# Turned features interleaved element by element, and one layer-0 vector held in a PSUM bank, in a four-layer graph-attention kernel

## The chip, the cores and the metric

The kernel runs on one core of a Trainium2 chip, in one launch. A core has five engines with instruction queues of their own: TensorE (PE: matrix products, results in PSUM), VectorE (DVE), ScalarE (ACT), GpSimd (POOL) and SyncE (SP), which here issues DMAs; 16 DMA engines move the data. SBUF is the working memory of 128 partitions, PSUM the small memory of 8 banks that TensorE writes. The metric is the device time of one execution in microseconds (us); lower is better.

## The reference

The input is 128 graphs of 128 nodes with 512 features each (`x`, float32) and a 0/1 adjacency matrix each (`adj`). Four layers follow, each `x = layernorm(x + attention(x, adj))`:

```
layer 0: scores = leaky(x.w_src + (x.w_dst)^T + b), softmax over neighbours, times x     (1 head, no projection)
layer 1: a two-stage attention: x @ W1 (512 x 1024, 4 heads of 256), elu, then @ W2 (1024 x 512, 1 head)
layer 2: 8 heads: x @ W (512 x 8*64), scores from a1 and a2, softmax, times the projection
layer 3: scores from x @ W_fc^T and W_attn, softmax, times x, elu                        (1 head)
```

All arithmetic is in float32.

## The kernel before

The kernel treats the graphs in pairs: 64 pairs, and `pair(n)` writes down the operations of one of them. `first` is layer 0, `second` and `third` are the two stages of layer 1, `fourth` is layers 2 and 3. Between them stand the projections with the weights `w1s`, `w2s` and `w3s`, which stay in SBUF.

Nothing is issued as it is written down. Each operation is a record with an engine, an estimated cost, the buffers that it reads and writes, and a due time. `plan` gives due times within a pair, spaced by `STRETCH`, and the pairs follow each other by `PACE`; `lay_out` then plays all engines forward in time by the estimated costs and writes out one fixed order for each engine's queue. It lets an operation run ahead of the oldest one not yet issued by at most `AHEAD`, gives out at most `BANKS` PSUM banks, counts a DMA by its cost and number of descriptors, and keeps DVE operations marked `port` from lying beside POOL's. Operations of several pairs are thus interleaved on each engine, and on the chip each engine works through its own fixed order, waiting on semaphores. `lay_out` also places the buffers in one SBUF `arena`.

A projection (`strassen`) multiplies the rows of two graphs by weights in seven block products instead of eight. Its left blocks, `left[g][a]`, are halves (a = 0 or 1) of the features of graph g, and four more are sums and differences of them that POOL makes (`sums`, line 853: eight of 128 x 256 in a pair for w1 and w3, four of 128 x 512 for w2). Three products use left blocks directly, four use the sums. Each block product is a chain of matmuls (line 829); each float32 matmul shows in the trace as two loads of weights (LDWEIGHTS, here the left block) and two MATMULs. A pair has 56, 56 and 28 such records for w1, w2 and w3. The other matmuls are L900 (attention times features, 12 records), L995 (32), L1057 (32) and L951 (2). The results leave PSUM by a copy (L837 on ACT, or L838 on DVE) or by an addition on DVE (L876).

TensorE needs the left operand with features on the partitions, so the features have to be turned. `turned` does it in three steps: DVE transposes blocks of 32 x 32 (line 726), one DMA writes them to DRAM (`scr`, line 730), and another reads them back with the blocks rearranged (line 734 or 739):

```python
op("SP", 0.7, lambda: nc.sync.dma_start(
    out=o.ap.rearrange("p h (q c) -> p h q c", q=4),
    in_=scr.ap.rearrange("p f -> (p f)").rearrange("(q p h c) -> p h q c", q=4, p=P, h=n),
), [scr], [o], dma=0.415 * n, desc=4 * P * n)
```

Each piece of this read is 32 float32, 128 bytes. The form with `ordered=True` turns the features of two graphs (8 tiles of 128 x 128, four for each graph) ahead of w1 and of w3: two calls in a pair. The first two pairs in layer 0, and the last one to three pairs in their later stages, are `quick`: they turn on TensorE (line 712) with a copy out of PSUM (line 720).

Layer 0's scores are four DVE instructions in a pair (line 940), two with `w0d` and two with `w0s`: each multiplies 128 x 512 features by a vector that is spread over all partitions, and sums. Both vectors are loaded into SBUF at the start by a DMA that repeats the row for every partition. Line 1023 adds `shift2` to two columns of scores, on DVE, before the scores of layer 1's second stage (line 753 on ACT, 766 on DVE).

Of the kernel before, what the change touches and what calls it, by code (L numbers as in the profile page):

```python
# [17 lines left out]
P = 128  # L18
# [7 lines left out]

STRETCH, PACE, AHEAD = 1.26, 44.3, 58.4
HOP = {"PE": 0.0, "DVE": 0.0, "ACT": 0.45, "POOL": 1.06, "SP": 2.0}
SEED, SPREAD = 1, 0.0
SETUP = (-36.3, -10.6, -19.3)  # L30
QUICK = (2, 0, 1, 2, 3)
FIRST, LAST = (-64.8, -62.4, -117.1, -110.8, -116.1), ()
BANKS, PRODUCTS = 8, 2
SEES = {"PE": 0.06, "DVE": 0.06, "ACT": 0.06, "POOL": 0.06, "SP": 0.0}
# [3 lines left out]
SLACK = 2.0  # L38
EXTRA = 0.2
FLEX = ("copy",)  # L40
REACH = 0.0
LOADS = (46.3, 7.8)

# [246 lines left out]
def tile_gat_stack(  # L290
# [65 lines left out]
    def lasting(shape, name):  # L356
        b = Buf("const", shape)
        b.ap = const.tile(shape, F32, name=name)
        return b
# [51 lines left out]

    begin[0] = SETUP[0]
    w0b = [lasting([P, F], n) for n in ("w0d", "w0s")]
    w0d, w0s = (b.ap for b in w0b)
    for b, w in zip(w0b, (w0_dst, w0_src)):
        load(-22, "ACT", lambda b=b: b.ap, w.partition_broadcast(P), b, 256)
    b0b = lasting([P, 1], "b0t")
# [218 lines left out]
    def part(b, *index):  # L636

        return b, lambda: b.ap[(slice(None), *index)]
# [3 lines left out]
    def spread(cols, split=1):  # L642
# [23 lines left out]
        for (b, col), k in cols:  # L666
            def turn(col=col, a=a, k=k):
                c, o = col(), sT.ap[:, a : a + k, :]
                if len(c.shape) > 2:
                    o = o.rearrange("p (a b) c -> p a b c", a=c.shape[1])  # L670
                nc.vector.transpose(o, c.unsqueeze(len(c.shape)).to_broadcast([*c.shape, 32]))

            op("DVE", 0.06 + 0.04 * k, turn, [b], joins=[sT])
            a += k
# [13 lines left out]
    def turned(srcs, n, moving=False, ordered=False):  # L688
# [3 lines left out]
        o = Buf(f"pt{n}", [P, 4, n, 32] if moving else [P, n, P])  # L692
        m = n // len(srcs)
        if quick[0]:
            for a, (b, src) in enumerate(srcs):
                if ordered:
                    own = Buf("own", [P, m, P])

                    def order(own=own, src=src, copy=(nc.vector.tensor_copy, nc.scalar.copy)[a % 2]):
                        copy(  # L700
                            own.ap.rearrange("p k (r b) -> p k r b", b=4),
                            src().rearrange("p k (b r) -> p k r b", b=4),
                        )

                    op(("DVE", "ACT")[a % 2], 0.06 + 0.137 * m, order, [b], [own])
                    b, src = own, lambda own=own: own.ap
                for lo in range(0, m, 4):
                    px, w = bank(), min(4, m - lo)

                    def flip(src=src, lo=lo, w=w, px=px):  # L710
                        for u in range(w):
                            nc.tensor.transpose(px.ap[:, u * P : (u + 1) * P], src()[:, lo + u, :], ident)  # L712

                    def taken(lo=a * m + lo, w=w, px=px, moving=moving, e=(lo // 4 + a) % 2):
                        if moving:
                            to = o.ap[:, :, lo : lo + w, :].rearrange("p q h c -> p h q c")
                            got = px.ap[:, : w * P].rearrange("p (h q c) -> p h q c", h=w, q=4)
                        else:
                            to, got = o.ap[:, lo : lo + w, :], px.ap[:, : w * P].rearrange("p (h i) -> p h i", h=w)
                        (nc.vector.tensor_copy, nc.scalar.copy)[e](to, got)  # L720

                    op("PE", 0.12 * w, flip, [b], [px])
                    op(("DVE", "ACT")[(lo // 4 + a) % 2], 0.06 + 0.137 * w, taken, [px], joins=[o])
            return o
        for a, (b, src) in enumerate(srcs):
# [19 lines left out]
    def attend(rows, src, mask, scaled=False):  # L745
# [33 lines left out]

        op("ACT", [0.4] * nh, prelu, [*dict.fromkeys(r[0] for r in rows), src[0]], [z])  # L780
        op("DVE", [0.24] * nh, masked, [z, mask[0]], [zz, nm])
        op("ACT", [0.387] * nh, exp, [zz, nm], [zz, rs])
# [10 lines left out]
    def norm(ys, plus=0.0):  # L793
# [8 lines left out]

        op("DVE", 0.15, both, [st], [mv])

# [31 lines left out]
    def copied(px, w, to, joins=(), outs=()):  # L836
        op("ACT", 0.04 + w / 1200, lambda: nc.scalar.copy(to(), px.ap[:, :w]), [px], outs, joins)  # L837
        either("copy", "DVE", 0.05 + w / 960, lambda: nc.vector.tensor_copy(to(), px.ap[:, :w]))  # L838

# [23 lines left out]
    def strassen(left, s, w, nk, wide, cols, to, out, ready):  # L863
# [11 lines left out]
        def added(px, u, g, h):  # L875
            op("DVE", 0.05 + wide / 960, lambda: nc.vector.tensor_add(to(g, h), px.ap[:, :wide], u.ap[:, :wide]), [px, u], joins=[out[g]])  # L876

# [27 lines left out]
    def resid(o, pa, ri, g, r):  # L905
        op("DVE", 0.645, lambda: nc.vector.scalar_tensor_tensor(
            out=o.ap, in0=pa.ap, scalar=ri.ap[:, g : g + 1], in1=r[1](), op0=ALU.mult, op1=ALU.add
        ), [pa, ri, r[0]], [o])
# [16 lines left out]
    def first(n):  # L925
# [11 lines left out]
        for s, wv, init in ((1, w0d, 0.0), (0, w0s, b0t)):  # L937
            for g in G:
                jk = Buf("junk", [P, F])
                op("DVE", 0.63, lambda g=g, s=s, wv=wv, init=init, jk=jk: nc.vector.tensor_tensor_reduce(  # L940
                    out=jk.ap, in0=x0.ap[:, g, :], in1=wv, scale=1.0, scalar=init, op0=ALU.mult, op1=ALU.add,
                    accum_out=sc0.ap[:, s, g : g + 1],
                ), [x0], [jk], joins=[sc0], uses=[*w0b, b0b], port=True)
            if s:
                rows = spread([(part(sc0, 1), 2)])
# [72 lines left out]
    def third(st, xl2):  # L1018
# [3 lines left out]
        rows = spread([(part(xl2, every, 0, F // 2), 2)])  # L1022
        op("DVE", 0.07, lambda: nc.vector.tensor_add(
            sc2.ap, xl2.ap[:, :, 1, F // 2], shift2.ap
        ), [xl2], [sc2], uses=[shift2], port=True)
        zz, ri = attend(rows, part(sc2), (m1, lambda h: m1.ap[:, h, :]))
# [8 lines left out]
    def fourth(n, st, xl3):  # L1035
# [10 lines left out]
        for g in G:  # L1046
# [4 lines left out]
            for q in range(2):  # L1051
# [21 lines left out]
            ), True)  # L1073
            op("DVE", 0.14, lambda g=g: nc.vector.tensor_reduce(
                out=sz.ap[:, g, :], in_=z3[g].ap[:, :, FO:].rearrange("p h s -> p s h"), op=ALU.add, axis=AX.X
# [29 lines left out]
        ), [y], [], dma=1.58, desc=2 * P)  # L1105

    quick = [False]

    def pair(n):
# [6 lines left out]
        xl = [Buf("xl1", [P, 2, N1]) for _ in G]  # L1116
        left = [[part(xT, slice(4 * g + 2 * a, 4 * g + 2 * a + 2)) for a in range(2)] for g in G]
        s = sums(left, [P, 2, P])
# [11 lines left out]
        xl3 = [Buf("xl3", [P, 2, C3]) for _ in G]  # L1130
        left = [[part(xT2, slice(4 * g + 2 * a, 4 * g + 2 * a + 2)) for a in range(2)] for g in G]
        strassen(left, sums(left, [P, 2, P]), w3s, 2, C3, slice(0, C3), lambda g, h: xl3[g].ap[:, h, :], xl3, wh_ready)
# [67 lines left out]
```

## Time and profile before

| | us |
|---|---|
| median of 3 runs | 2966.2 (2963.7 to 2967.05) |
| the profiled execution | 2964.05 |
| its span, first to last instruction | 2962.3 |
| PE busy | 2892.2 |
| PE loading weights (beside matmuls) | 2360.1 |
| DVE busy | 2762.8 |
| ACT busy | 2326.7 |
| POOL busy | 2213.1 |

The granted TensorE clock was 0.991 over the span. The DMA engines moved 588.18 MB in 1448819 packets, 1236740 of them under 512 bytes. A group row of the profile gives line, engine, operation, tiles and shapes, count, busy time, mean duration in nanoseconds of one instruction, and idle time before it with what ended it. Mean durations overlap where an engine pipelines, so they can be longer than the spacing of the instructions. A row of the chain of waits or of the timeline gives start, length, engine, line and how many instructions are merged in it.

### The profile page before, as it was taken

How to read it: one execution, taken by the hardware profiler on the slowest of the kernel's cores; microseconds unless marked ns; L12 is line 12 of the kernel's file. 1: busy time of each engine (PE TensorE's matmuls, PEld its weight loads, DVE VectorE, ACT ScalarE, POOL GpSimd, SP SyncE). 2: the span in 40 equal slices, each digit the busy share in tenths (PEclk: the TensorE clock that was granted, in tenths of full speed). 3: DMA queues.
4: the chain of work that ended last, by engine and by line, in shares of the span. 5: the costliest groups of instructions: out<-in, count | busy, mean ns of one | idle time of the engine just before them, and what ended most of it. 6: DMA issues, size and time to landing. Idle time of an engine off the chain costs nothing. (4 is left out here: it accounts for less than half of the span.)

```text
span 2962.3 us, 56920 instructions
## 1 busy us (share of the span) xinstructions
PE 2892.2 (98%) x14292; PEld 2360.1 (80%) x14292; DVE 2762.8 (93%) x9694; ACT 2326.7 (79%) x7795; POOL 2213.1 (75%) x2855
## 2 busy tenths in 40 slices
PE   7999999999999999999999999999999999999997
PEld 4878788888888888888888888888888888888885
DVE  7789899999999999999999999999999999999976
ACT  3467788788788788788788788788778778778778
POOL 3877777777777877877877877877877877777854
PEclk9999999999999999999999999999999999999998
DMA  4369899999999999999999999999999999999851
GB/s 136 85 165 208 194 220 216 209 218 214 213 212 212 211 212 212 212 209 213 215 208 212 214 207 215 214 208 217 211 204 219 213 204 219 212 204 217 195 118 43
DMA packets 1448819, 588.18 MB, mean 199 GB/s; under 512 B 1236740, under 2 KB 1351172, under 8 KB 1448492
## 3 DMA queue, kind: packets, MB, share of 16 engines
q1 hardware_dynamic: 1447416, 582.97, 86.4%
q8 instruction: 116, 1.90, 0.3%
q14 instruction: 211, 1.73, 0.2%
q10 hardware_dynamic: 1076, 1.58, 0.2%
HBM read 363.68 MB, written 220.75 MB: 197 GB/s over the span
## 5 line engine op out<-in xcount | busy, mean ns | idle before, releaser
L829 PE MATMUL ps<-w2s,arena 128*128 128x257 f32 x3584 | 834.5, 384 | 3.6 <-DVE arena L1003 2.1
L829 PE MATMUL ps<-w1s,arena 128*128 128x258 f32 x3584 | 807.4, 383 | 6.5 <-DVE arena L876 3.2
L829 PEld LDWEIGHTS ps<-w1s,arena 128*128 128x128 f32 x3584 | 680.6, 190 | 162.1 <-issue 43.0
L775 ACT ACTIVATE arena<-arena,nm 128x128 f32<-128x128 f32 x1920 | 741.3, 389 | 62.2 <-DVE nm L766 58.5
L853 POOL TENSOR_TENSOR arena<-arena 128x256 f32<-128x256 f32 (+1 forms) x768 | 694.4, 922 | 114.2 <-DVE arena L1003 49.9
L829 PEld LDWEIGHTS ps<-w2s,arena 128*128 128x128 f32 x3584 | 667.8, 190 | 119.1 <-POOL arena L853 18.2
L753 ACT ACTIVATE ps<-arena 128x128 f32<-128x128 f32 x1480 | 538.7, 370 | 53.9 <-DMA arena<-row 15.0
L726 DVE STREAM_TRANSPOSE arena<-arena 128x512 f32<-128x512 f32 (+1 forms) x803 | 497.3, 630 | 24.8 <-ACT arena L775 4.6
L766 DVE CUSTOM_DVE_ANT_0 arena<-ps,arena 128x128 f32<-128x128 f32 x1850 | 501.8, 379 | 13.9 <-ACT ps L753 10.2
L829 PE MATMUL ps<-w3s,arena 128*128 128x273 f32 x1792 | 471.7, 398 | 20.7 <-DVE arena L876 16.5
L817 ACT ACTIVATE arena<-arena,mr,rd 128x512 f32<-128x512 f32 x512 | 393.7, 809 | 50.5 <-POOL mr L813 50.5
L829 PEld LDWEIGHTS ps<-w3s,arena 128*128 128x128 f32 x1792 | 322.2, 190 | 98.7 <-DVE arena L876 36.8
L837 ACT COPY arena<-ps 128x257 f32<-128x257 f32 (+2 forms) x577 | 205.4, 375 | 245.4 <-PE ps L829 245.1
L900 PE MATMUL ps<-arena 128*128 128x512 f32 x768 | 376.7, 602 | 3.2 <-DVE arena L720 2.9
L775 ACT ACTIVATION_READ_ACCUMULATOR arena<-arena,nm 128x1 f32 x1920 | 361.8, 188 | 0.0
L984 POOL TENSOR_TENSOR arena<-arena,b1t 128x512 f32<-128x512 f32 x256 | 349.8, 1371 | 10.8 <-DVE b1t L500 3.3
L797 DVE BATCH_NORM_STATS2 st<-arena 128x6 f32<-128x512 f32 x512 | 336.2, 678 | 9.3 <-POOL arena L1068 4.6
L876 DVE TENSOR_TENSOR arena<-ps,arena 128x258 f32<-128x258 f32 (+2 forms) x768 | 306.0, 412 | 35.3 <-PE ps L829 18.4
L812 POOL TENSOR_TENSOR md<-mv,rd 128x2 f32<-128x2 f32 x256 | 54.0, 211 | 374.3 <-ACT rd L807 357.3
L911 POOL TENSOR_SCALAR arena<-arena 128x256 f32<-128x256 int32 x256 | 292.2, 1141 | 54.8 <-DMA arena<-in_adj_dram 14.9
L766 DVE DVE_READ_ACCUMULATOR2_ANT nm<- 128x1 f32 x1850 | 278.5, 151 | 0.0
L1057 PEld LDWEIGHTS ps<-arena 128*128 128x128 f32 x2048 | 249.8, 194 | 33.9 <-issue 27.7
(97 smaller groups left out, 3952.8 us busy)
## 6 DMA issues: line engine op xcount, KB each, us to landing
scr<-arena SPq DMA_DIRECT2D x309, 512.0 KB
arena<-scr SPq DMA_DIRECT2D x309, 512.0 KB
arena<-row SPq DMA_DIRECT2D x185, 512.0 KB
arena<-in_x_dram SPq DMA_DIRECT2D x64, 512.0 KB
out_dram<-arena SPq DMA_DIRECT2D x64, 512.0 KB
arena<-row SPq DMA_DIRECT2D x185, 128.0 KB
scr<-arena SPq DMA_DIRECT2D x185, 128.0 KB
arena<-scr SPq DMA_DIRECT2D x185, 128.0 KB
```

Of the source, the lines that this page charges most:

```text
L726: op("DVE", 0.075 + 0.134 * m, lambda a=a, src=src: nc.vector.transpose(zb.ap[:, :, a * m : (a + 1) * m, :].rearrange("p b h c -> p h b c" ...
L753: nc.scalar.activation(z.ap[:, h * P : (h + 1) * P], rows[h][1](), AF.Prelu, bias=src[1]()[:, h : h + 1], alpha=SLOPE)
L766: nc.vector.tensor_tensor_reduce(out=zz.ap[:, h, :].rearrange("p (b a) -> p a b", b=4), in0=z.ap[:, h * P : (h + 1) * P].rearrange("p (a b ...
L775: nc.scalar.activation(zz.ap[:, h, :], zz.ap[:, h, :], AF.Exp, bias=nm.ap[:, h : h + 1], scale=-1.0, accum_out=rs.ap[:, h : h + 1],)
L797: op("DVE", 0.585, lambda g=g, y=y: nc.vector.bn_stats(st.ap[:, g, :], y()), [b], joins=[st])
L817: op("ACT", 0.715, lambda g=g, y=y: nc.scalar.activation(y(), y(), AF.Identity, bias=mr.ap[:, g : g + 1], scale=rd.ap[:, g : g + 1]), [b, ...
L829: nc.tensor.matmul(px.ap[:, :w], lhsT=lhs(k), rhs=rhs(k), start=(fresh and k == 0), stop=(k == nk - 1), skip_group_check=True,)
L853: op("POOL", cost, lambda: nc.gpsimd.tensor_tensor(out=own[o][1](), in0=a[1](), in1=b[1](), op=what), [a[0], b[0]], [s[o]])
L876: op("DVE", 0.05 + wide / 960, lambda: nc.vector.tensor_add(to(g, h), px.ap[:, :wide], u.ap[:, :wide]), [px, u], joins=[out[g]])
L900: op("PE", 0.885, lambda: nc.tensor.matmul(pa.ap.rearrange("p (s c) -> p s c", s=2) if paired else pa.ap, lhsT=pt.ap[:, h, :], rhs=xv[1]() ...
L911: op("POOL", 1.25, lambda: nc.gpsimd.tensor_scalar(out=m.ap, in0=a.ap, scalar1=0.0, scalar2=-BIG, op0=what, op1=ALU.mult), [a], [m])
L984: op("POOL", 1.255, lambda g=g, c=c: nc.gpsimd.tensor_add(xl[g].ap[:, c, : 2 * FH], xl[g].ap[:, c, : 2 * FH], b1t[:, c * 2 * FH : (c + 1) ...
```

## The change

- The turned features of one graph's `ordered` tiles are interleaved: instead of four tiles of 128 x 128 one after the other, the buffer is `[P, graph, node, k]` with the tile number k innermost. DVE's transpose writes that order (a step of four elements, 16 bytes, within a row), and the read from DRAM moves pieces of 128 elements, 512 bytes.
- The left blocks become views of this buffer (`halves`): both TensorE's loads of weights and POOL's sums read it at a step of 16 bytes. The quick form writes its copies at that step.
- `w0d` is no longer spread over SBUF by a DMA: its row is loaded, TensorE spreads it with a matmul against ones into a PSUM bank, and it stays there. `BANKS` falls from 8 to 7. The two line-940 instructions that use it are no longer marked `port`.
- Line 1023's addition becomes an ACT instruction.
- The planner's constants change: `PACE`, `AHEAD`, `EXTRA` and a number of estimated costs, so the order of all queues is made anew.

```diff
-STRETCH, PACE, AHEAD = 1.26, 44.3, 58.4
+STRETCH, PACE, AHEAD = 1.26, 44.0, 70.0
-BANKS, PRODUCTS = 8, 2
+BANKS, PRODUCTS = 7, 2
-EXTRA = 0.2
+EXTRA = 0.5
...
-    w0b = [lasting([P, F], n) for n in ("w0d", "w0s")]
-    w0d, w0s = (b.ap for b in w0b)
-    for b, w in zip(w0b, (w0_dst, w0_src)):
-        load(-22, "ACT", lambda b=b: b.ap, w.partition_broadcast(P), b, 256)
+    w0b = [Buf("const", [P, F]), lasting([P, F], "w0s")]
+    w0d = w0b[0].ap = psum.tile([P, F], F32, name="w0d")
+    w0s = w0b[1].ap
+    r0 = row(-22, "ACT", one_row(w0_dst), F)
+    load(-22, "ACT", lambda: w0s, w0_src.partition_broadcast(P), w0b[1], 256)
+    at(-20, "PE", 0.9, lambda: nc.tensor.matmul(w0d, lhsT=ones[0:1, :], rhs=r0.ap[0:1, :], start=True, stop=True), [r0], [w0b[0]])
...
+        if ordered:
+
+            zb, o = Buf(f"zb{n}", [P, 4, len(srcs), 32 * m]), Buf(f"pt{n}", [P, len(srcs), P, m])
...
+                        elif ordered:
+                            to, got = o.ap[:, lo // m].rearrange("p i k -> p k i"), px.ap[:, : w * P].rearrange("p (h i) -> p h i", h=w)
...
+        if ordered:
+            for a, (b, src) in enumerate(srcs):
+                op("DVE", 0.075 + 0.134 * m, lambda a=a, src=src: nc.vector.transpose(
+                    zb.ap[:, :, a, :].rearrange("p b (c k) -> p k b c", k=m),
+                    src().rearrange("p h (b c) -> p h b c", c=32),
+                ), [b], joins=[zb])
+            op("SP", 0.5, lambda: nc.sync.dma_start(
+                out=scr.ap, in_=zb.ap.rearrange("p b a e -> p (b a e)")
+            ), [zb], [scr], dma=0.05 + 0.19 * n, desc=P)
+            op("SP", 0.6, lambda: nc.sync.dma_start(
+                out=o.ap.rearrange("p a (q c) k -> p a q (c k)", q=4),
+                in_=scr.ap.rearrange("p f -> (p f)").rearrange("(q p a e) -> p a q e", q=4, p=P, a=len(srcs)),
+            ), [scr], [o], dma=0.22 * n, desc=4 * P * len(srcs))
+            return o
...
-        op("ACT", [0.4] * nh, prelu, [*dict.fromkeys(r[0] for r in rows), src[0]], [z])
-        op("DVE", [0.24] * nh, masked, [z, mask[0]], [zz, nm])
+        op("ACT", [0.345 if nh < 4 else 0.378] * nh, prelu, [*dict.fromkeys(r[0] for r in rows), src[0]], [z])
+        op("DVE", [0.234] * nh, masked, [z, mask[0]], [zz, nm])
...
-                ), [x0], [jk], joins=[sc0], uses=[*w0b, b0b], port=True)
+                ), [x0], [jk], joins=[sc0], uses=[w0b[1 - s], b0b], port=not s)
...
-        op("DVE", 0.07, lambda: nc.vector.tensor_add(
-            sc2.ap, xl2.ap[:, :, 1, F // 2], shift2.ap
-        ), [xl2], [sc2], uses=[shift2], port=True)
+        op("ACT", 0.2, lambda: nc.scalar.activation(
+            sc2.ap, xl2.ap[:, :, 1, F // 2], AF.Identity, bias=shift2.ap[:, 0:1]
+        ), [xl2], [sc2], uses=[shift2])
...
+    def halves(t):
+
+        return [[(t, lambda g=g, a=a: t.ap[:, g, :, 2 * a : 2 * a + 2].rearrange("p i k -> p k i")) for a in range(2)] for g in G]
...
-        left = [[part(xT, slice(4 * g + 2 * a, 4 * g + 2 * a + 2)) for a in range(2)] for g in G]
+        left = halves(xT)
...
-        left = [[part(xT2, slice(4 * g + 2 * a, 4 * g + 2 * a + 2)) for a in range(2)] for g in G]
+        left = halves(xT2)
```

Six further estimated costs of DVE and ACT operations change by up to 0.055 us.

More of the change, by code (lines that the diff above doesn't have):

```diff
@@ L23 @@
 FMAX = 3.0e38
-STRETCH, PACE, AHEAD = 1.26, 44.3, 58.4
-HOP = {"PE": 0.0, "DVE": 0.0, "ACT": 0.45, "POOL": 1.06, "SP": 2.0}
+STRETCH, PACE, AHEAD = 1.26, 44.0, 70.0
+HOP = {"PE":0.0,"DVE":0.0,"ACT":0.45,"POOL":1.06,"SP":2.0}
 SEED, SPREAD = 1, 0.0
-SETUP = (-36.3, -10.6, -19.3)
-QUICK = (2, 0, 1, 2, 3)
-FIRST, LAST = (-64.8, -62.4, -117.1, -110.8, -116.1), ()
-BANKS, PRODUCTS = 8, 2
+SETUP = (-36.3,-10.6,-19.3)
+QUICK = (2,0,1,2,3)
+FIRST, LAST = (-64.8,-62.4,-117.1,-110.8,-116.1), ()
+BANKS, PRODUCTS = 7, 2
 SEES = {"PE": 0.06, "DVE": 0.06, "ACT": 0.06, "POOL": 0.06, "SP": 0.0}
@@ L38 @@
 SLACK = 2.0
-EXTRA = 0.2
+EXTRA = 0.5
 FLEX = ("copy",)
 REACH = 0.0
-LOADS = (46.3, 7.8)
+LOADS = (46.3,7.8)
 class Buf:
@@ L671, in turn @@
                 nc.vector.transpose(o, c.unsqueeze(len(c.shape)).to_broadcast([*c.shape, 32]))
-            op("DVE", 0.06 + 0.04 * k, turn, [b], joins=[sT])
+            op("DVE", 0.08 + 0.04 * k, turn, [b], joins=[sT])
             a += k
@@ L801, in both @@
                 nc.vector.bn_aggr(mv.ap[:, g, :], st.ap[:, g, :])
-        op("DVE", 0.15, both, [st], [mv])
+        op("DVE", 0.18, both, [st], [mv])
         def root():
@@ L836, in copied @@
     def copied(px, w, to, joins=(), outs=()):
-        op("ACT", 0.04 + w / 1200, lambda: nc.scalar.copy(to(), px.ap[:, :w]), [px], outs, joins)
-        either("copy", "DVE", 0.05 + w / 960, lambda: nc.vector.tensor_copy(to(), px.ap[:, :w]))
+        op("ACT", 0.05 + w / 1200, lambda: nc.scalar.copy(to(), px.ap[:, :w]), [px], outs, joins)
+        either("copy", "DVE", 0.065 + w / 960, lambda: nc.vector.tensor_copy(to(), px.ap[:, :w]))
     def project(lhs, wa, nk, w, n, to, t, ready):
@@ L875, in added @@
         def added(px, u, g, h):
-            op("DVE", 0.05 + wide / 960, lambda: nc.vector.tensor_add(to(g, h), px.ap[:, :wide], u.ap[:, :wide]), [px, u], joins=[out[g]])
+            op("DVE", 0.075 + wide / 960, lambda: nc.vector.tensor_add(to(g, h), px.ap[:, :wide], u.ap[:, :wide]), [px, u], joins=[out[g]])
         first = len(ops)
@@ L905, in resid @@
     def resid(o, pa, ri, g, r):
-        op("DVE", 0.645, lambda: nc.vector.scalar_tensor_tensor(
+        op("DVE", 0.7, lambda: nc.vector.scalar_tensor_tensor(
             out=o.ap, in0=pa.ap, scalar=ri.ap[:, g : g + 1], in1=r[1](), op0=ALU.mult, op1=ALU.add
@@ L1073, in fourth @@
             ), True)
-            op("DVE", 0.14, lambda g=g: nc.vector.tensor_reduce(
+            op("DVE", 0.09, lambda g=g: nc.vector.tensor_reduce(
                 out=sz.ap[:, g, :], in_=z3[g].ap[:, :, FO:].rearrange("p h s -> p s h"), op=ALU.add, axis=AX.X
```

## Prediction

> **What bounds the kernel now.** I read the page's busy rows first, for the engine with least room, then a table by windows for the steady middle.
>
> ```profile
> PE 2892.2 (98%) x14292; PEld 2360.1 (80%) x14292; DVE 2762.8 (93%) x9694; ACT 2326.7 (79%) x7795; POOL 2213.1 (75%) x2855
> q1 hardware_dynamic: 1447416, 582.97, 86.4%
> ```
> ```profile
> core 0: us, PE busy (x) PEld busy (x) DVE busy (x) ACT busy (x) POOL busy (x), PEclk, DMA share, GB/s
> 1044.00:1488.00 444.00, 439.86 (x2185) 360.56 (x2184) 429.77 (x1504) 360.87 (x1217) 341.64 (x441) 1.00 0.93 212
> ```
> Three resources are nearly full in the middle: PE 99%, DVE 97%, the DMA engines 93%; ACT (81%) and POOL (77%) have room. A busy PE row is modelled, so I take PE's true beat from the chain of waits, whose end is nearly all PE:
>
> ```profile
> 2699.74 2.11 PE ps L829 x8
> 2704.48 1.72 PE ps L900 x4
> 2706.20 2.62 PE ps L1057 x24
> 2715.82 8.70 PE ps L829 x40
> 2729.71 2.68 PE ps L995 x24
> 2732.39 1.85 PE ps L829 x8
> 2743.99 2.11 PE ps L829 x8
> ```
> The first and last lines are the same place one pair of graphs later: 44.25 us per pair. The beats: w1 products (x40) 217.5 ns, w3 (x8 at 2732) 231, L900 430 ns, L995 112 ns, L1057 109 ns; the w2 products, not shown, do 24 in 5.27 us, 220 ns. Per pair 56 x 0.2175 + 56 x 0.220 + 28 x 0.231 + 12 x 0.430 + 32 x 0.112 + 32 x 0.109 + 0.2 (L951) = 43.4 us. So PE has 0.85 us of idle in 44.25, and no change that leaves the matmuls alone can win more than 0.85 x 64 = 54 us in the steady part.
>
> Where the idle lies, the timeline shows at one of some 35 like places (the waits of the steady middle put 12.8 us in 35 times to this pair of lines):
>
> ```profile
> 1546.99 1.72 POOL L984 TENSOR_TENSOR arena<-arena,b1t 128x512 f32<-128x512 f32 x1
> 1547.51 0.43 DVE L876 TENSOR_TENSOR arena<-ps,arena 128x273 f32<-128x273 f32 x1
> 1547.87 1.40 DVE L940 CUSTOM_DVE_ANT_0 arena<-arena,w0s,b0t 128x512 f32<-128x512 f32 x1
> 1547.99 1.45 PEld L829 LDWEIGHTS ps<-w3s,arena 128*128 128x128 f32 x7 [0.79 <-DVE arena L876]
> 1547.99 1.65 PE L829 MATMUL ps<-w3s,arena 128*128 128x273 f32 x6 [0.39 <-DVE arena L876]
> ```
> Another L940, from 1545.91, had run 1.67 us beside POOL; L876 was queued behind it on DVE, and PE waited for L876. By groups:
>
> ```profile
> L940 DVE CUSTOM_DVE_ANT_0 arena<-arena,w0s,b0t 128x512 f32<-128x512 f32 x128 | 178.8, 1401 | 1.8 <-PE ps L375 1.8
> L940 DVE CUSTOM_DVE_ANT_0 arena<-arena,w0d 128x512 f32<-128x512 f32 x128 | 142.3, 1147 | 5.5 <-DMA arena<-in_x_dram 5.5
> L1023 DVE TENSOR_TENSOR sc<-arena,shift 128x2 f32<-128x2 f32 x64 | 26.2, 410 | 0.1
> L1003 DVE SCALAR_TENSOR_TENSOR arena<-arena,ps 128x512 f32<-128x512 f32 x256 | 167.4, 674 | 8.1 <-ACT arena L1002 8.1
> L853 POOL TENSOR_TENSOR arena<-arena 128x256 f32<-128x256 f32 x512 | 357.7, 715 | 50.1 <-DMA arena<-scr 15.5 <-ACT arena L775 12.1 <-DVE arena L876 5.1
> L1057 PEld LDWEIGHTS ps<-arena 128*128 128x128 f32 x2048 | 249.8, 194 | 33.9 <-issue 27.7 <-DVE arena L720 0.7 <-DVE ri L783 0.5
> ```
> L940, both inputs in SBUF, costs 1147 and 1401 ns, against 674 for L1003, as wide, with one input in PSUM. The extra is waiting for POOL: the w0d form's median is 692, so half its instances don't meet POOL at all.
>
> **The change part by part**, per pair unless said.
>
> DVE loses lock waits. With w0d in PSUM its two L940 have one SBUF input: 2 x (1147 - 690) = 0.91 us gone. L1023 leaves DVE: 0.41, of which about 0.26 was waiting (a tiny DVE instruction, L783, takes 150). ACT gets it at about 0.2 (L807: 203 ns); behind it on ACT stand only that layer's L753, which needed it anyway, and ACT idles 8 us a pair. The w0s pair stays: 2 x (1401 - 692) = 1.42 us of waits. So 1.17 of 2.59 us of waits go, 45%, and DVE falls by 1.3 us from 42.8 (429.77 of 444, times 44.25).
>
> Layout on DVE. The two ordered transposes (L726, 692 ns) now write at a 16-byte step. The nearest row is L766, which writes at a 128-byte step: the trace has it at 233 ns from start to start, and its unit-step twin L761 at 211. 22 ns per 128 elements is 88 per transpose, 0.18 a pair at most; at least 0, as nothing else in it changes. I take 0.1.
>
> DMA. The two reads back move 2048 pieces of 512 B instead of 8192 of 128 B. In the trace's packet records a 128 B packet takes 16.5 ns and one of 512 B 31.9: 8192 x 16.5 / 16 = 8.4 us against 4.1. The DMA share falls from 93% to about 84%. Of itself that is worth 0: in the middle PE waits for no DMA. SP's issues stay as many (about 0.6 us each), and fewer descriptors can only release SP earlier.
>
> TensorE's weights. Three of seven Strassen products (both left blocks and the last) load straight from the turned tile: 24 of w1's 56 loads and 12 of w3's 28 now step by 16 bytes. No load of before steps so. What a load costs today: L1057 moves 66 columns and L995 128, yet both beat at 109 to 112 ns, so there the load sets the beat and takes about 109; the 190 in the rows is latency. In the products it hides under 217.5 and 231. The Trainium skill, "SBUF — State Buffer", Specifications, speaks against the change: a 16-byte line needs two hits for full bandwidth, and here each element is alone on its line. At half rate a load takes about 2 x 107 + 2 = 216 ns: still under 217.5, so by this rule too the sum is 0, except where a strided load follows a short matmul (+0.1 each, up to 0.3 a pair). By the contiguous row it is 0. Below nothing it cannot be. If the cover goes, at three times, 24 x 110 + 12 x 96 = 3.8 us a pair. I take 0.05.
>
> POOL's sums (L853, eight of 256) now read both or one input at that step. The rows have only 715 ns contiguous; L1068, reading 64 of every 66, is no slower than its like. The skill's "GPSIMD Engine Reference", Performance pitfalls, gives about 50% more per element for steps over 8 bytes. By the row nothing; by the rule 0.36 each, 2.9 us of POOL (34.0 to 36.9 of 44), and the fourth sum 1.4 later. What hides it: near 1032 us the w1 products start at 1032.25, the one that uses the last sum comes 16 matmuls on, at 1035.73, and that sum is done by 1034.1: 1.6 us of room. Near 1004 and 1050 us the w3 sums have over 3. I take the rule, and it fits: 0 on the path. At double time (+2.8 us) PE would wait about 1.2 a pair.
>
> One PSUM bank goes for good: 7 are left for 3-bank products, two at a time, plus scores. The trace doesn't show a wait for a bank by name. From below 0; from above one more stall a pair like the 0.46 above. I take 0.05.
>
> The order. New costs, PACE, AHEAD and EXTRA let all queues be ordered anew, SP's and POOL's too; no row prices that. It can give back or take some tenths of a us a pair; I take 0 and keep it in the range.
>
> At the start w0d's broadcast becomes a 2 KB row, a matmul (L375, 0.8 us) and PE at a queue that already waits to 7.1 us: within 1 us either way. In the first two and last pairs the ordered copies (L720, 580 to 690 ns) write at the new step: under 1 us together.
>
> The sum. I read PE's idle as DVE's lateness, so that it shrinks as DVE's lost time does. DVE is freed of 1.17 us of waits and 0.15 of L1023's own work and given 0.1 for the transposes: 1.22 of 2.59, 47%. 0.47 x 0.85 = 0.40 us; less 0.05 for the loads and 0.05 for the bank, 0.30; over 64 pairs 19 us. The profiled execution was 2964.05 (span 2962.3, 1.75 around it), 2.15 under the median of the runs shown; so 2945 on its scale and 2947 on the median's.
>
> **Rivals.**
> (1) The loads bind: slower. Place: the 36 strided loads; it decides from 217 ns a load, twice today's, on. At three times +3.8 us a pair: about 3190; at 235 ns 24 x 17 + 12 x 4 = 0.46 a pair, +29 against the gain: about 2976. For: a step that leaves one element per line, and a margin of 1.5 ns at half rate. Against: [...]L766's writes show one line per element costing DVE almost nothing. 10% for a large loss, 8% for a small one.
> (2) Banks, or sums later than their room: PE waits 0.5 to 1.2 us a pair, less the gain: 2979 to 3024. For: PE's order is fixed, and one late operand stalls it. Against: ACT's and DVE's drains follow PE within a microsecond. 17%.
> (3) Nothing: the remaining stall is behind a w0s L940, which still meets POOL, so the DVE time is freed where PE didn't wait: 2962 to 2970. 8%.
> (4) All of PE's idle goes: 2966 - 54, about 2912. 5%, part of faster.
>
> **How the numbers follow.** The likeliest case has 52% at 2947 (its own range 2922 to 2960), with (4) 57% faster. A measurement of this kernel tells about 0.2% (6 us) from no change; within it 8%. Slower 35%: (1) 18, (2) 17. Range 2915 to 3000: about 5% lies below, and the large losses of (1) and the worst of (2), 13%, above.
>
> **What would show it.** Right: L940 with w0d near 690 ns, no DVE L1023, DVE under 95% in the middle, DMA share near 0.84, loads of w1s with a beat of 217.5 still, L853 of 256 near 1.0 us without PE waiting for it, a pair every 43.9 to 44.0 us. Wrong: w1 runs of matmuls with beats above 220 ns; PE waits before L829 on POOL L853, or on copies that free a bank; a pair in 44.3 us or more.

## The result: slower by 3.5%, and the profile after

The changed kernel takes 3067.9 us (median of 4 runs, 3067.4 to 3068.9) against 2965.0 (4 runs, 2963.0 to 2967.1) for the kernel before on the same chip. The ratio is 1.0347, with a 95% interval of 1.0333 to 1.0361: 103 us slower, where 2947 was forecast. Its profiled execution has a span of 3065.6 us.

The page of the kernel after, its busy rows and its DMA row:

```profile
PE 2948.2 (96%) x14294; PEld 2482.6 (81%) x14294; DVE 2717.4 (89%) x9576; ACT 2367.3 (77%) x7913; POOL 2246.2 (73%) x2855
q1 hardware_dynamic: 1066488, 582.97, 71.2%
```

The table by windows, the same stretch of the steady middle as before:

```profile
core 0: us, PE busy (x) PEld busy (x) DVE busy (x) ACT busy (x) POOL busy (x), PEclk, DMA share, GB/s
1044.00:1488.00 444.00, 434.39 (x2122) 367.63 (x2122) 407.63 (x1451) 354.43 (x1188) 337.02 (x430) 1.00 0.77 205
```

This is the puzzle of the case. Every engine is *less* busy than before: DVE's share fell from 97% to 92%, the DMA engines' from 93% to 77%, and yet fewer matmuls get done in the same 444 us (2122 against 2185). The granted clock is full in both. Part of the fall is only the longer pair; DVE's busy time for one pair still fell, from 42.5 us to 41.6 by the records. PEld alone rose: loads of weights take longer.

The groups of the kernel after, by form. L851 is the products' matmul (L829 before), L875 POOL's sums (L853), L735 the ordered transposes, L748 the others, L962 the layer-0 products (L940), L1045 the addition that was L1023:

```profile
L851 PEld LDWEIGHTS ps<-w1s,arena 128*128 128x128 f32 x3584 | 753.7, 248 | 212.2 <-DVE arena L1118 39.9 <-DVE arena L898 28.7 <-issue 23.8
L851 PEld LDWEIGHTS ps<-w2s,arena 128*128 128x128 f32 x3584 | 673.4, 190 | 102.0 <-DVE w2s L402 2.4 <-issue 2.3 <-DVE arena L860 0.9
L875 POOL TENSOR_TENSOR arena<-arena 128x256 f32<-128x256 f32 x512 | 446.5, 893 | 46.5 <-DMA arena<-scr 10.7 <-ACT ps L775 7.8 <-DVE arena L728 6.5
L735 DVE STREAM_TRANSPOSE arena<-arena 128x512 f32<-128x512 f32 x248 | 276.0, 1113 | 7.4 <-ACT arena L839 3.7
L748 DVE STREAM_TRANSPOSE arena<-arena 128x512 f32<-128x512 f32 x370 | 254.3, 694 | 10.8 <-POOL arena L807 3.3 <-ACT arena L797 2.4 <-POOL sc L1107 0.5
L962 DVE CUSTOM_DVE_ANT_0 arena<-arena,w0s,b0t 128x512 f32<-128x512 f32 x128 | 152.3, 1202 | 2.1 <-PE ps L375 2.1
L962 DVE CUSTOM_DVE_ANT_0 arena<-arena,w0d 128x512 f32<-128x512 f32 x128 | 83.0, 673 | 3.8 <-DMA arena<-in_x_dram 3.7
L1045 ACT ACTIVATE sc<-arena,shift 128x2 f32<-128x2 f32 x64 | 18.1, 282 | 6.5 <-DVE arena L898 6.5
```

The loads of w1s and the transposes before:

```profile
L829 PEld LDWEIGHTS ps<-w1s,arena 128*128 128x128 f32 x3584 | 680.6, 190 | 162.1 <-issue 43.0 <-ACT ps L753 11.8 <-DVE arena L876 5.5
L726 DVE STREAM_TRANSPOSE arena<-arena 128x512 f32<-128x512 f32 x618 | 423.3, 692 | 19.8 <-ACT arena L775 1.9 <-ACT arena L817 1.8 <-DVE arena L726 1.0
```

Read them in pairs. The ordered transposes take 1113 ns, where the others, as wide but writing at unit step, take 694. There are 248 of them: four a pair of graphs in the steady part. The loads of w1s, of which 24 in 56 step by 16 bytes, have a mean of 248 ns, while those of w2s, all at unit step, have 190: from these two means a strided load has a latency of about 325 ns, an estimate. The sums went from 715 to 893 ns, and that mean hides three kinds. By their order in POOL's queue, the first of each four (both inputs at the step, the two halves of one graph, whose elements lie within the same 16 bytes) takes 664 ns in the records, the second and fourth (one such input) 868, the third (both inputs at the step, from two graphs) 1172; before they took 731, 693, 736 and 698. L962 with w0d did just what it was changed for: 1147 to 673.

What PE waits for between 600 and 2376 us, by the waits of PE (total us, times, longest):

```profile
PE ps L851 <- DVE arena L1118: 17.5, 19, 1.6
PE ps L851 <- DVE arena L898: 8.7, 17, 1.1
PE ps L851 <- DVE arena L860: 4.6, 12, 0.7
PE ps L851 <- ACT ps L775: 2.9, 6, 1.0
```

Before, one pair of lines held nearly all of it (13.2 us in all):

```profile
PE ps L829 <- DVE arena L876: 12.8, 35, 0.5
```

Now there are several kinds, 35.8 us with the smaller ones, and longer waits. (These lists leave out waits of 150 ns and less.) L898, L860 and L1118 each read a PSUM bank and write nothing that a product reads: PE waits for a bank that DVE has not emptied yet. L1118 (L1096 before) belongs to the last layer of an earlier pair, and no such line is in before's list. So two kinds of loss are seen: steps that became longer, and queues whose order fits less well. The runs were chosen to part them.

To locate the loss I divide each span at the first w1 product of pair 3 and of pair 63, the pairs counted from 0 (from the trace's records; us):

| kernel | up to pair 3 | 60 pairs | per pair | after pair 63 |
|---|---|---|---|---|
| before | 139.2 | 2664.0 | 44.40 | 159.0 |
| after | 150.9 | 2743.6 | 45.73 | 171.2 |

Of 103 us, 80 are in the steady part, 1.33 a pair; 12 are lost at the start and 12 at the end. In the steady part PE's busy time went from 43.94 to 44.62 us a pair and its idle time, short gaps included, from 0.46 to 1.10: about half of the loss is longer matmul work, half is waiting.

### The profile page after: what moved, and what is told of

The parts are those of the page before. It is cut to its first block, busy times and chain, and to the rows that moved or that the text cites. A ratio compares the mean times of both kernels' runs of the same rounds, so it can differ in the third digit from the quotient of the medians.

```text
span 3065.6 us, 57246 instructions
## 1 busy us (share of the span) xinstructions
PE 2948.2 (96%) x14294; PEld 2482.6 (81%) x14294; DVE 2717.4 (89%) x9576; ACT 2367.3 (77%) x7913; POOL 2246.2 (73%) x2855
## 4 chain that ended last, share of the span: by engine, by line
PE 46%; DVE 16%; ACT 12%; POOL 6%; issue 5%; DMA 4%; SPq 0%; DVEq 0%; ACTq 0%; POOLq 0%
PE ps L851 33%; PE ps L1017 6%; ACT ps L775 5%; ACT arena L797 4%; PE ps L922 4%; PE ps L1079 4%; DVE arena L788 3%; DVE st L819 2%; DMA arena<-row 2%; DVE arena L748 2%; POOL arena L875 2%; DVE arena L735 2%; ACT arena L839 1%; DVE arena L928 1%; POOL arena L1006 1%
## 5 line engine op out<-in xcount | busy, mean ns | idle before, releaser
L851 PEld LDWEIGHTS ps<-w1s,arena 128*128 128x128 f32 x3584 | 753.7, 248 | 212.2 <-DVE arena L1118 39.9
L851 PE MATMUL ps<-w1s,arena 128*128 128x258 f32 x3584 | 866.0, 395 | 61.3 <-DVE arena L1118 24.4
L875 POOL TENSOR_TENSOR arena<-arena 128x256 f32<-128x256 f32 (+1 forms) x768 | 765.7, 1016 | 208.1 <-DVE arena L1025 69.8
L851 PE MATMUL ps<-w2s,arena 128*128 128x257 f32 x3584 | 823.2, 381 | 2.7 <-DVE w2s L402 2.3
L851 PEld LDWEIGHTS ps<-w2s,arena 128*128 128x128 f32 x3584 | 673.4, 190 | 102.0 <-DVE w2s L402 2.4
L859 ACT COPY arena<-ps 128x257 f32<-128x257 f32 (+2 forms) x631 | 232.2, 374 | 335.1 <-PE ps L851 311.6
L851 PE MATMUL ps<-w3s,arena 128*128 128x273 f32 x1792 | 473.6, 404 | 3.7 <-DVE arena L1025 1.6
L851 PEld LDWEIGHTS ps<-w3s,arena 128*128 128x128 f32 x1792 | 377.9, 245 | 47.7 <-DVE arena L898 7.3
L898 DVE TENSOR_TENSOR arena<-ps,arena 128x258 f32<-128x258 f32 (+2 forms) x768 | 301.5, 416 | 99.0 <-PE ps L851 80.5
L748 DVE STREAM_TRANSPOSE arena<-arena 128x256 f32<-128x256 f32 (+1 forms) x555 | 333.5, 606 | 23.0 <-ACT arena L797 13.4
L1006 POOL TENSOR_TENSOR arena<-arena,b1t 128x512 f32<-128x512 f32 x256 | 328.0, 1291 | 2.0 <-ACT arena L859 1.1
L933 POOL TENSOR_SCALAR arena<-arena 128x256 f32<-128x256 int32 x256 | 275.9, 1078 | 23.6 <-ACT ps L775 2.0
L735 DVE STREAM_TRANSPOSE arena<-arena 128x512 f32<-128x512 f32 x248 | 276.0, 1113 | 7.4 <-ACT arena L839 3.7
```

What stands on the lines that cost most here:

```text
L735: op("DVE", 0.075 + 0.134 * m, lambda a=a, src=src: nc.vector.transpose(zb.ap[:, :, a, :].rearrange("p b (c k) -> p k b c", k=m), src().re ...
L748: op("DVE", 0.075 + 0.134 * m, lambda a=a, src=src: nc.vector.transpose(zb.ap[:, :, a * m : (a + 1) * m, :].rearrange("p b h c -> p h b c" ...
L851: nc.tensor.matmul(px.ap[:, :w], lhsT=lhs(k), rhs=rhs(k), start=(fresh and k == 0), stop=(k == nk - 1), skip_group_check=True,)
L875: op("POOL", cost, lambda: nc.gpsimd.tensor_tensor(out=own[o][1](), in0=a[1](), in1=b[1](), op=what), [a[0], b[0]], [s[o]])
L1006: op("POOL", 1.255, lambda g=g, c=c: nc.gpsimd.tensor_add(xl[g].ap[:, c, : 2 * FH], xl[g].ap[:, c, : 2 * FH], b1t[:, c * 2 * FH : (c + 1) ...
```

## The experiments

Two theories. One: the steps at 16 bytes cost the time (DVE's transposes, TensorE's loads, POOL's sums, each to be undone by itself). The other: the planner made another order from the new constants, costs and number of banks, and that order is the worse one, whatever the steps cost. A third: the eighth PSUM bank is missed. In the expectations the letters L (TensorE's loads), D (DVE's transposes) and S (all steps) stand for forms of the first, O (the order) and C (the constants) for forms of the second, and B (the bank) for the third.

### The steps undone in the new order

These four keep the changed kernel's order and its 512-byte pieces, and take the step away from one engine each, and from all three. TensorE's loads read the same bytes as contiguous tiles:

```diff
+    def flat_halves(t):
+        return [[(t, lambda g=g, a=a: t.ap[:, g].rearrange("p i k -> p (i k)")[:, 2 * P * a : 2 * P * (a + 1)].rearrange("p (k i) -> p k i", k=2)) for a in range(2)] for g in G]
...
-            strassen(left, s, w1s, 2, C1, cols, lambda g, h, cols=cols: xl[g].ap[:, h, cols], xl, w1_ready)
+            strassen(flat_halves(xT), s, w1s, 2, C1, cols, lambda g, h, cols=cols: xl[g].ap[:, h, cols], xl, w1_ready)
...
```

> The changed kernel, with TensorE alone loading the left blocks of w1 and w3 at unit step (the same buffer read as four contiguous tiles, so the products are of other numbers; all else, and the order of every queue, is the same). Theory L (the strided loads: the trace shows a beat of 233 ns where it was 217): 36 loads get back 16 or 4 ns each, 0.43 us a pair, so 28 us: about 3040; more if late products also delay others. Theory D (DVE's transposes at the new step): no more than that, 3040 to 3068. Theory O (the new order and seven banks): about 3060.

Measured: 3053.7 us, 1.0294 (1.0276 to 1.0311). TensorE's step is worth some 16 us by the ratios (1.0347 less 1.0294), not the 28 of its theory: PE's busy time falls by 0.53 us a pair, and its idle time rises by 0.28 (1.10 to 1.38), with its listed waits going from 35.8 to 45.5 us. It comes earlier to what it waits for, and waits longer.

DVE's transposes write at unit step:

```diff
-                    zb.ap[:, :, a, :].rearrange("p b (c k) -> p k b c", k=m),
+                    zb.ap[:, :, a, :].rearrange("p b (k c) -> p k b c", k=m),
```

> The changed kernel, with DVE's ordered transposes (L735) writing runs of 32 as before (the tiles then hold other numbers; order unchanged). Theory D: L735 falls from 1113 to about 692 ns, four in a pair, 1.7 us of DVE a pair, and PE, which waits behind DVE's L1118, L898 and L860, gets most of it back: 2985 to 3010. Theory L: under 10 us, about 3060. Theory O: about 3050, as DVE had room (92% busy).

Measured: 3038.4 us, 1.0239 (1.0224 to 1.0255): 32 us, the largest of the three, between what the theories said. PE's waits in the window fall from 35.8 to 21.6 us.

POOL's sums read contiguous tiles:

```diff
-        s = sums(left, [P, 2, P])
+        s = sums(flat_halves(xT), [P, 2, P])
...
```

> The changed kernel, with POOL's sums alone reading contiguous tiles (other numbers; order unchanged). The sums of 256 go from 893 to about 715 ns, eight in a pair. All theories: PE hardly waits on POOL (4.5 us in 5 waits of the weight loads in the steady part), so 3060 to 3068. If it falls below 3050, the sums were on the path.

Measured: 3064.3 us, 1.0327 (1.0312 to 1.0343): the intervals of this and of the changed kernel overlap, so at most a few us.

All three edits together:

> All three at unit step at once, order unchanged, DRAM pieces still of 512 bytes. Theories D and L together: all of the loss and something of the hoped-for gain comes back, 2940 to 2965. Theory O: the new order with seven banks still costs, 2985 to 3030.

Measured: 3011.7 us, 1.0149 (1.0134 to 1.0164). The three give back about 59 us together, close to their sum (54). But 44 us stay, with no step left in the kernel: the first theory is true and is only some 57% of the answer. The waits of PE in this last kernel, in the same window:

```profile
PE ps L851 <- DVE arena L898: 10.3, 17, 1.2
PE ps L851 <- DVE arena L1118: 10.1, 19, 0.9
PE ps L851 <- DVE arena L860: 4.0, 10, 0.6
```

They are at the places of the changed kernel, L1118 again 19 times, but shorter (10.1 us, not 17.5); the other two are much as they were. All its waits are 31.6 us, 18.4 more than before's, or about 0.46 for each of the window's 40 pairs; its pair takes 44.78, 0.38 more than before's. The steps are gone and the waits stay: the places come with the order.

### The layout alone, in the old order

Here the kernel before gets the layout, with the old costs, DMA estimate and descriptor count told to the planner, so that each engine's sequence of instructions is exactly before's (in the trace, on TensorE, DVE, ACT and POOL):

```diff
+        if ordered:
...
+            op("SP", 0.7, lambda: nc.sync.dma_start(
+                out=o.ap.rearrange("p a (q c) k -> p a q (c k)", q=4),
...
+            ), [scr], [o], dma=0.415 * n, desc=4 * P * n)
+            return o
...
-        left = [[part(xT, slice(4 * g + 2 * a, 4 * g + 2 * a + 2)) for a in range(2)] for g in G]
+        left = halves(xT)
```

> The kernel before with the turned layout alone, planned at the old costs, so that every engine's order, the eight banks and w0d stay exactly as before: only the steps in memory and the DRAM pieces of 512 bytes differ. Theory S (the steps themselves cost what the runs with single steps undone gave back, about 56 us together): 3015 to 3035. Theory O (most of the loss is the new order, the steps find room in a good one): 2970 to 2995. If the 512-byte pieces help: lower by as much.

Measured: 3015.7 us, 1.0178 (1.0161 to 1.0194). The steps cost 53 us in the old order too. The table by windows, the transposes, and PE's waits of this kernel (L732 the ordered transposes, L848 the products, L895 before's L876):

```profile
1044.00:1488.00 444.00, 437.44 (x2148) 374.45 (x2147) 433.11 (x1484) 355.87 (x1189) 351.45 (x437) 1.00 0.79 209
L732 DVE STREAM_TRANSPOSE arena<-arena 128x512 f32<-128x512 f32 x248 | 277.1, 1117 | 10.3 <-ACT arena L836 1.4 <-DVE arena L732 0.5
PE ps L848 <- DVE arena L895: 23.8, 38, 0.9
PE ps L848 <- DVE arena L857: 0.4, 1, 0.4
```

The first wait is the one of before at the same pair of lines, now 23.8 us instead of 12.8: DVE, at 97.5%, is later with the same work. That is 0.28 us more a pair. The chain of waits shows the other half:

```profile
2701.08 2.24 PE ps L848 x8
2717.29 8.94 PE ps L848 x40
2762.30 8.94 PE ps L848 x40
2807.36 12.54 PE ps L848 x56
```

The x40 run was 8.70 before, and is 223.5 ns a matmul instead of 217.5; x56 was 12.18 in before's chain. In the records a w1 product with a strided load comes 233 ns after the one ahead of it, where a unit one comes after 217; a w3 product with one takes 233 to 234 against 229. That makes 24 x 16 + 12 x 4 ns = 0.43 us a pair. A run of eight after a wait is longer by 0.13 too (2.24 against 2.11), about what the estimate above gives as one load's extra latency. The waits' 0.28 and the loads' 0.43 make 0.71 of the 0.76 that a pair takes more here (45.16 against 44.40).

Then the steps are taken away one after the other, in this same order. First DVE's, by the edit shown above:

> The layout alone in the old order (3016 us), with DVE's ordered transposes writing runs of 32 (the tiles hold other numbers). If DVE, which is 97% busy in that order, is what the layout hits: 1.7 us of DVE a pair come back, 2975 to 2990, and what is left is TensorE's loads, 28 us at most. If TensorE's loads are the larger part: 3000 or more.

Measured: 2983.4 us, 1.0050 (1.0034 to 1.0066). Then TensorE's and POOL's as well, which leaves the 512-byte pieces as the one difference from before:

> The layout alone in the old order with DVE, TensorE and POOL all at unit step (other numbers in the tiles): only the DRAM pieces of 512 instead of 128 bytes are left. If the DMA relief was off the path: 2958 to 2968. If it helps: below 2955.

Measured: 2967.5 us, 0.9995 (0.9987 to 1.0004). First the window and PE's waits of the kernel with DVE at unit step, then window, transposes and sums of the one with no step:

```profile
1044.00:1488.00 444.00, 441.66 (x2173) 377.25 (x2173) 425.04 (x1484) 358.03 (x1202) 351.06 (x439) 1.00 0.81 210
PE ps L848 <- DVE arena L895: 3.5, 15, 0.4
PE ps L848 <- DVE arena L857: 1.4, 2, 0.9
```
```profile
1044.00:1488.00 444.00, 440.18 (x2186) 360.57 (x2185) 429.81 (x1504) 360.31 (x1214) 339.66 (x440) 1.00 0.81 212
L732 DVE STREAM_TRANSPOSE arena<-arena 128x512 f32<-128x512 f32 x248 | 172.0, 694 | 11.9 <-ACT arena L836 2.2 <-DVE arena L732 0.5
L872 POOL TENSOR_TENSOR arena<-arena 128x256 f32<-128x256 f32 x512 | 357.0, 713 | 42.1 <-DVE arena L745 11.3 <-DMA arena<-scr 10.5 <-DVE arena L895 3.9
```

By the ratios, DVE's step is worth 38 us (33 by the spans, 3012.6 and 2979.6), TensorE's and POOL's together 16, the pieces nothing. The DMA share fell from 93% to 81% in the last kernel and the time stayed: DMA was off the path.

DVE's 38 us are less than its extra work. In the records an ordered transpose holds DVE about 936 ns, from its start to the next instruction's, instead of 625; four make 1.24 us a pair; only 0.48 of it came through (45.16 less 44.67). PE waits for DVE hold it: 24.2 us in the window with the step, 4.9 without, 19.3 over 40 pairs = 0.48. And in the kernel with DVE at unit step, TensorE's step still in, PE waits less than before's 12.8 us, so part of the loads' 0.43 fills time that was idle: 0.28 a pair came through (44.67 less 44.39).

### The new order, piece by piece

The rest, 44 to 50 us of 103, has to come from what else changed. In these kernels the planner does more than order: for each of the 1024 copies out of PSUM (L837 on ACT, L838 on DVE) it also chooses the engine, by the estimated costs and `EXTRA`. Before, DVE makes 447 of them, in the changed kernel 393, and each remade plan below divides them anew. Where this text says order, it means this division too. The layout is undone altogether; the constants, costs, w0d's bank and L1023's move stay:

```diff
-        left = halves(xT)
+        left = [[part(xT, slice(4 * g + 2 * a, 4 * g + 2 * a + 2)) for a in range(2)] for g in G]
...
```

> The changed kernel with the turned layout undone altogether (tiles one after the other, DRAM pieces of 128 bytes, the read planned at its old cost), and its constants, w0d in PSUM and seven banks kept. Both theories: within 25 us of the changed kernel with all three steps at unit stride (3012), as the pieces of 512 bytes are off the path. If the DMA relief is worth something, it is slower than 3012.

Measured: 2982.9 us, 1.0051 (1.0034 to 1.0069). This is 15 us, not 44 as in the kernel with unit steps, and just outside what was expected: without the new cost of the DMAs the planner makes yet another order, with other waits. Its up-to-pair-3 part is 149.3, so most of the loss at the start stays.

The kernel before with one bank less, nothing else:

```diff
-BANKS, PRODUCTS = 8, 2
+BANKS, PRODUCTS = 7, 2
```

> The kernel before with one number changed: seven PSUM banks to plan with instead of eight (the eighth stays empty). Theory B (the bank is the cost: with every step at unit stride the changed kernel is still 45 us slow, with PE waiting behind DVE's and ACT's drains of banks): 2985 to 3015. Theory C (the new constants make the order worse, the bank does little): 2960 to 2975.

Measured: 2956.3 us (7 runs), 0.9965 (0.9954 to 0.9977): faster by 11 us, outside both theories. A plan with seven banks need not be slower, so nothing speaks for the third theory here. But the order is remade with the number, and an order moves the time by more than that (below), so this run doesn't price the bank itself, and in the changed kernel it wasn't tried. Its L940 rows tell something else:

```profile
L940 DVE CUSTOM_DVE_ANT_0 arena<-arena,w0s,b0t 128x512 f32<-128x512 f32 x128 | 134.8, 1057 | 1.6 <-PE ps L375 1.6
L940 DVE CUSTOM_DVE_ANT_0 arena<-arena,w0d 128x512 f32<-128x512 f32 x128 | 97.0, 765 | 5.3 <-DMA arena<-in_x_dram 5.3
```

With w0d still in SBUF it went from 1147 to 765, because in this order it meets POOL less often: POOL was at work when it began in 16 of 128 cases, in the kernel before in 68, and the others take about 685 ns in the mean in both. Most of what the change bought with a bank, another order gives for nothing.

The kernel before with w0d in PSUM, 7 banks, L1023 on ACT, as in the diff of the change, and AHEAD 57.5:

> The kernel before with w0d in PSUM, seven banks and line 1023 on ACT, and nothing else (AHEAD 57.5 instead of 58.4, so that the buffers fit). Theory B: within 10 us of the one with seven banks alone; the DVE time that is freed (1.3 us a pair) gives back at most 20 us. Theory C: it gains what was forecast, 2935 to 2955.

Measured: 2988.4 us, 1.0071 (1.0054 to 1.0087), outside both theories. Its groups (L943 is L940):

```profile
L943 DVE CUSTOM_DVE_ANT_0 arena<-arena,w0s,b0t 128x512 f32<-128x512 f32 x128 | 191.1, 1522 | 2.6 <-PE ps L375 2.6
L943 DVE CUSTOM_DVE_ANT_0 arena<-arena,w0d 128x512 f32<-128x512 f32 x128 | 82.6, 680 | 3.7 <-DMA arena<-in_x_dram 3.7
```

w0d's wait went, and the w0s form, not touched, became longer (1401 to 1522). At the start 6 us are lost (145.2 up to pair 3), with the old constants.

The kernel before with the new constants and costs of DVE and ACT, 8 banks, w0d in SBUF, and AHEAD 68:

```diff
-STRETCH, PACE, AHEAD = 1.26, 44.3, 58.4
+STRETCH, PACE, AHEAD = 1.26, 44.0, 68
...
-EXTRA = 0.2
+EXTRA = 0.5
...
-        op("DVE", [0.24] * nh, masked, [z, mask[0]], [zz, nm])
+        op("DVE", [0.234] * nh, masked, [z, mask[0]], [zz, nm])
...
```

> The kernel before with the changed kernel's constants and estimated costs alone: PACE 44.0, AHEAD 68 (70 doesn't fit in SBUF beside w0d), EXTRA 0.5, eight banks, layout and w0d as before. Theory B: 2950 to 2975. Theory C: 2985 to 3015, with some 20 us of it at the start and the end, where the changed kernel of unit steps is that much later.

Measured: 2995.2 us, 1.0092 (1.0075 to 1.0109): 27 us from numbers that only the planner reads. Of it 8 are at the start and 7 at the end. PE waits for a bank here too, with all eight to choose from, behind one DVE instruction (L1003) in every pair:

```profile
PE ps L829 <- DVE arena L1003: 38.5, 40, 1.3
```

That is more than its pair lost (44.61 against 44.40), so other lost time of PE went; the waits that the list names are not all of it.

How far an order moves the time by itself is measured with the kernel before and another seed, a random term in the planner's priorities:

```diff
-SEED, SPREAD = 1, 0.0
+SEED, SPREAD = 3, 0.3
```

> The kernel before with SPREAD 0.3 and SEED 3: each operation's due time is moved by a random 0 to 0.3 us before the orders are made, nothing else. Theory O (any change of the plan's inputs draws a new order, worth a per cent either way): 2950 to 3010, most likely slower than 2967. Theory C (the changed constants were worse for a reason of their own): within 10 us of 2967.

Measured: 2974.8 us, 1.0039 (1.0024 to 1.0054), which fits both theories. With seed 5:

> The same with SEED 5: another draw of the order. Theory O: 2950 to 3010 and more than 6 us from the draw with SEED 3. Theory C: within 10 us of 2967.

Measured: 3027.5 us, 1.0215 (1.0200 to 1.0230), beyond what either theory said. The same work, with no cost of any operation changed, is 12 and 64 us slower; 103 and 50 of the copies moved from ACT to DVE as well. What PE waits for with seed 5 are lines that it hardly waited for before:

```profile
PE ps L829 <- ACT arena L837: 17.2, 27, 0.8
PE ps L829 <- POOL arena L853: 6.2, 11, 0.7
```

If an order is bad because the planner was told false costs, true ones should mend it. The changed kernel with the measured costs of transposes, sums and strided loads, AHEAD 66:

```diff
-                op("DVE", 0.075 + 0.134 * m, lambda a=a, src=src: nc.vector.transpose(
+                op("DVE", 0.075 + 0.234 * m, lambda a=a, src=src: nc.vector.transpose(
...
-        cost = {256: 0.66, 512: 1.255}[s[0].size]
+        cost = {256: 0.85, 512: 1.255}[s[0].size]
```

> The changed kernel, the planner told what was measured: 1.01 us for an ordered transpose instead of 0.61, 0.85 for a sum instead of 0.66, 0.466 instead of 0.436 for a strided w1 matmul (AHEAD 66 so that the buffers fit). If the order was late because of wrong costs: 3000 to 3030, what is left being the work of the steps. If orders are draws, anything from 3020 to 3090.

Measured: 3027.6 us, 1.0205 (1.0184 to 1.0226), some 42 us better than the changed kernel and still slower than the layout in the old order. Since two seeds lie 52 us apart, one such order, which fits both expectations, doesn't show that the true costs were the reason.

Last, w0d in PSUM in a held order: the kernel with 7 banks, its order kept, and w0d's row spread by one matmul into the bank that is free there:

```diff
-BANKS, PRODUCTS = 8, 2
+BANKS, PRODUCTS = 7, 2
...
+    def w0d_spread():
+        nc.scalar.dma_start(out=w0r, in_=one_row(w0_dst))
+        nc.tensor.matmul(w0d, lhsT=ones[0:1, :], rhs=w0r, start=True, stop=True)
+
+    at(-22, "ACT", 0.5, w0d_spread, [], [w0b[0]], 256 / 190.0)
...
```

> The kernel with seven banks (2956 us) with w0d spread by TensorE into the eighth bank, every order otherwise exactly that kernel's. In it the L940 of w0d takes 765 ns in the mean, so by theory O the placement is worth at most 2 x 0.1 us a pair: 2942 to 2958. If it is slower by over 10 us, reading the vector from PSUM has a cost of its own.

Measured: 2949.5 us, 0.9954 (0.9939 to 0.9969). Its two forms (L947 is L940):

```profile
L947 DVE CUSTOM_DVE_ANT_0 arena<-arena,w0s,b0t 128x512 f32<-128x512 f32 x128 | 142.0, 1112 | 2.5 <-PE ps L375 2.5
L947 DVE CUSTOM_DVE_ANT_0 arena<-arena,w0d 128x512 f32<-128x512 f32 x128 | 86.0, 679 | 3.6 <-DMA arena<-in_x_dram 3.6
```

It beats the kernel before and the changed one. Against the 7-bank kernel the difference is 3 us by the ratios, and the two intervals overlap: in that order, which had taken most of the wait away already, no worth of w0d in PSUM is shown.

## Why the prediction was wrong

**The sum.** The steps cost 53 us in the old order and 59 in the new, where 0.15 a pair (10 us) had been taken for them. The other 44 to 50 us are what the new order and the rest cost; 0 had been put. A gain of 0.40 a pair was expected on top; no run shows it as the work of w0d or of L1023.

**The two ordered transposes, 0.1 us: the step that failed first.** Two things were wrong in it. It counted two a pair; the trace has four. And it chose as the nearest row an operation of another kind, L766, which writes at a 128-byte step and is 22 ns slower per 128 elements from start to start. The transpose is 311 ns slower per 512 from start to start (936 against 625), 78 per 128, and 421 by duration (1113 against 692). Four make 1.24 us a pair by their starts, on the engine that had 3% of room; 32 to 38 us of the 103 are theirs. L766 and the transpose are both on DVE and both write far apart; a row of another operation was no bound.

**The loads, 0.05 us.** The Trainium skill ("SBUF — State Buffer", Specifications) says that at least two hits on a 16-byte line are needed for full bandwidth and that each new line costs something; it gives no rate. Half rate, and with it 216 ns, was the prediction's own reading, and its split of the measured 109 ns into 107 and 2 stands in no row: twice 109 is 218, already more than the 217.5 that was to cover it. 233 was measured, so a cost there is, as the page says. The prediction had worked out the price past its margin of 1.5 ns (235 ns: 0.46 a pair). Measured were 0.43 in matmul time, 0.28 in the period. This was rival (1) in its small form; taking 0.05 was a choice for the cheap side of an edge.

**POOL's sums, 0.** The skill's "GPSIMD Engine Reference", Performance pitfalls for Q7 kernels, has about 50% more for such reads. In the mean it was 25% (893 against 715), and no one figure fits: the three kinds are 9% less, 25% more and 59% more. That the sums hide in their room held nearly: undoing their step moved the time by 4 to 6 us, near the noise.

**DMA, 0, and the bank, 0.05.** DMA was right: the pieces alone give 0.9995. The share in the middle was 0.81 in the old order and 0.77 in the changed kernel, whose pair takes longer, not 0.84. The bank's 0.05 was a guess that nothing contradicts; no run prices it, as the order was remade with it.

**w0d and L1023.** The mechanism held: 1147 to 673 where 690 was put, no L1023 on DVE, 282 ns on ACT. The inference from it failed: "PE's idle is DVE's lateness, so that it shrinks as DVE's lost time does". In the changed kernel DVE is at 92%, less than before, and PE's waits for it are larger. With each queue in a fixed order, PE waits for one certain instruction, and what stands ahead of that one decides, not only how full the engine is. Three of the prediction's signs of being right (w0d's form near 690 ns, no L1023 on DVE, DVE under 95%) came true in a slower kernel: they were signs of DVE's load, not of PE's time.

**The order: "I take 0 and keep it in the range", some tenths of a us a pair.** That is the term most mis-sized. The seeds put it at 12 and 64 us. The remade orders that carry an edit came to 27 (the constants alone), 21 (w0d with its bank and L1023), 15 (the change without its layout) and -11 (a bank less): six in all, and all but one of them losses. The range, 2915 to 3000, would have reached to most of these orders alone, but not to the steps (3016 in the old order) nor to both.

**Rivals.** Rival (1) in its small form came true for the loads, at the price worked out for it. Rival (2)'s sign is there as well: PE waits on instructions that free a bank, and its listed waits are 35.8 us against 13.2, about 0.6 a pair more, inside its 0.5 to 1.2. DVE's lateness is a part of it, as undoing DVE's step took 14 us of these waits; whether one more bank would have helped isn't shown. The prediction let either rival happen and not both.

**What stays open.** That the steps cost 53 us and that 44 us remain with no steps is shown. That those 44 are the order is argued, not shown: one of two seeds shows that an order can cost as much, and the pieces and w0d are free where the order was held, but the bank and L1023's move weren't run by themselves in a held order. About 11 of them fall before pair 3 and 12 after pair 63, 23 in the steady part of the kernel with unit steps. Which of AHEAD, EXTRA, PACE or the costs spoils start and end wasn't parted, nor the sequence from the division of copies between ACT and DVE, nor what makes one order better than another. Nor was an eighth bank given back to the changed kernel.

## What to carry to other kernels

Where a planner writes the order anew, price the draw first: run the old kernel with two other seeds, and hold the old order when you want to know what an edit is worth. For an operation whose access pattern changes, take no bound from another operation, count its instances in the groups, and where its cover is within one per cent of the estimate, count it as paid. An engine's share of busy time didn't say who would be waited for: the lines of the waits did.

## What the hardware showed that I had not expected

- DVE's transpose of 128 x 512 (fp32) takes 1113 ns when it writes at a 16-byte step and 692 at unit step, about 936 and 625 from its start to the next instruction's; the accumulating operation at L766 and its 128-byte step cost 233 against 211 ns for 128 elements. Why the two differ so isn't known from these runs.
- With a load of weights that takes one fp32 element per 16 bytes, the next w1 product begins only after 233 ns, where 217 was the beat and is again with the step undone; the load's latency is about 325 ns against 190, by estimate.
- POOL's addition or subtraction of 256 elements takes 1172 ns when both inputs are read at that step and lie apart, 868 with one such input, and 664 when both are read at it but lie within the same 16 bytes, less than the 731 of the same one at unit step.
- Making the pieces in DRAM four times larger took the DMA engines' share from 93% to 81% in the same order, and nothing beyond the noise from the time (0.9995, 0.9987 to 1.0004).
